# Preparing the next batch item in TensorE's gaps, with routing spread over the attention loop

## The chip, the cores and the metric

The kernel runs on one core of a Trainium2 chip. The metric is the device time of one execution, in microseconds. The kernel before takes 2810.74 us (median of three runs, 2806.79 to 2811.39). The profiled execution has a span of 2745.2 us on the trace and 2746.91 us as a run.

## The reference

Eight items of 256 channels by 1024 positions (32 x 32) pass through two layers, all in f32. Layer 0 is an attention with 8 heads of 64, whose softmax runs over the query axis (`axis=1`). Layer 1 is a single-head attention on a layer norm, and then a mixture of 8 experts, of which each token takes two.

```python
# layer 0
xt = x.reshape(B, C, S).transpose(0, 2, 1)
qkv = (xt @ w_qkv + b_qkv).reshape(B, S, N_HEADS, 3 * D_K)
q, k, v = jnp.split(qkv, 3, axis=-1)
attn = jnp.einsum('bihd,bjhd->bijh', q, k) * SCALE
attn = jax.nn.softmax(attn, axis=1)
res = jnp.einsum('bijh,bjhd->bihd', attn, v).reshape(B, S, N_HEADS * D_K)
x = res @ w_out + b_out + xt
# layer 1
t = t + attention(ln(t), W)           # scores (ln(t) W^T) ln(t)^T, softmax over the last axis
n = ln(t)
probs = softmax(n @ router_w.T); rw, re = top_k(probs, 2); rw = rw / rw.sum(-1)
out = n + sum_e combine[:, e] * (gelu(n @ w1[e] + b1[e]) @ w2[e] + b2[e])
t = t + out
```

## The kernel before

The items are worked on one after the other. Items 0 to 6 are routed: their normed rows are scattered by expert into a table in HBM, and the experts run on all of them together, after layer 0 of item 7. Item 7 itself goes through all eight experts densely. For each item, `layer0`, `attend` and `dispatch` follow each other.

The first part of layer 0 makes the values (4 parts of 2 blocks) and the queries and keys of the first pair of heads. `big` is a PSUM tile of 128 x 1024 f32, and its pool has three buffers; `acc` is 128 x 512, and its pool has two.

```python
def project(b, xT, g, t):                       # t = 0: queries, 1: keys
    pq = big(f"pqk_{b}_{g}_{t}")
    for cc in range(NCC):
        for n in range(NH2):
            nc.tensor.matmul(pq[:, ts(n, 512)], wqkv[:, cc, t, ts(g, P)],
                             xT[:, cc, ts(n, 512)], start=(cc == 0), stop=(cc == NCC - 1))
    dst = two.tile([P, S], F32, tag=f"qk{t}", ...)
    evicted[b, g, t] = nc.vector.tensor_scalar(
        dst, pq, b_qk[:, t, g : g + 1], SCALE if t == 0 else 1.0, ALU.add, ALU.mult)

def values(b, xT):
    v = one.tile([P, NT, INNER], F32, tag="v", name=f"v_{b}")
    for i in range(0, NT, 2):
        pv = big(f"pv_{b}_{i}")
        ...                                     # 4 matmuls 128x128 by 128x512
        for j in range(2):
            nc.vector.tensor_add(v[:, i + j, :], pv[:, ts(j, 512)], b_v)
```

Then come 32 steps (4 pairs of heads by 8 blocks of keys). Each step has two heads `h`; the scores of a head fill a `big` tile in two halves of 512. Two matmuls of 64 rows on different halves of the array run together: the first half of one head's scores beside the second half of the other's. The maximum is taken in two instructions, one for each half; the second continues from the first and gives the bias of the exponential, which also sums its rows.

```python
for at in range(last + LAG + 1):                # LAG = 2
    if at <= last:
        score(at, 0, 0)                         # head 0, first half
    if 0 < at <= last + 1:
        score(at - 1, 1, 1)                     # head 1 of the step before, second half
        soften(at - 1, 1)                       # second max, exponential, 1/sum, vs = v / sum
    if at <= last:
        first_max(at, 0)
        score(at, 0, 1)
        score(at, 1, 0)
        soften(at, 0)
        first_max(at, 1)
    if at >= LAG:
        gather_values(at - LAG)                 # 4 matmuls po <- vs, ex
    if at <= last:
        if g + 1 < NPAIR and j in (3, 5):       # next pair of heads
            qks[g + 1].append(project(b, xT, g + 1, len(qks[g + 1])))
```

After the loop the output projection (`pr`, 8 blocks) gives `t1`. `attend` norms it, transposes it, multiplies with W and runs 8 blocks of attention:

```python
layer_norm(t1, n1, 1e-5, f"a{b}")               # bn_stats, Sqrt on ScalarE, reciprocal, 8 tensor_scalar
to_channels(n1, nT, f"n1_{b}")                  # 16 transposes on TensorE, 2 copies on VectorE
... px -> xa                                    # 8 matmuls
def mix(i, ex, ssum):
    pt = big(f"pa_{b}_{i}")
    ...                                         # 8 transposes of ex
    nc.vector.tensor_copy(aT, pt)
    py = acc(f"py_{b}_{i}")
    ...                                         # 8 matmuls aT x n1
```

`dispatch` norms and transposes again, computes the router's logits with 16 matmuls of 128x8 and then, on small tiles of 128x64 and 128x8, softmax, the two best experts and the row of each token. Two matmuls count rows (`pc` before this token, `pn` in all), in two `acc` tiles. 16 indirect DMAs then scatter the rows.

```python
layer_norm(t2, n2, 1e-5, f"f{b}")
to_channels(n2, nT, f"n2_{b}")
gate, hots = gates(b, nT)                       # logits, Exp on ScalarE, some 20 small VectorE operations
both = hots[0] + hots[1]
pc = before^T both ; pn = ones^T both           # two matmuls, acc tiles
... per, upto (scan), rows, counts
for k in range(2): ... row, exp, to, at         # 6 small VectorE operations each
16 x nc.gpsimd.indirect_dma_start(rows at `at` <- n2)
nc.gpsimd.tensor_add(t2, t2, n2)
nc.sync.dma_start(group.sums[...], t2)
```

Of the kernel before, what the change touches and what calls it, by code (L numbers as in the profile page):

```python
# [10 lines left out]
F32 = mybir.dt.float32  # L11
# [7 lines left out]
def kernel(  # L19
# [23 lines left out]
    nc = tc.nc  # L43
# [241 lines left out]

    def values(b, xT):
        v = one.tile([P, NT, INNER], F32, tag="v", name=f"v_{b}")
        for i in range(0, NT, 2):
            pv = big(f"pv_{b}_{i}")
            for j in range(2):  # L290
                for cc in range(NCC):
                    nc.tensor.matmul(  # L292
                        pv[:, ts(j, 512)],
                        xT[:, cc, ts(i + j, P)],
                        wqkv[:, cc, 2, :],
                        start=(cc == 0),
                        stop=(cc == NCC - 1),
                    )
            for j in range(2):
                nc.vector.tensor_add(v[:, i + j, :], pv[:, ts(j, 512)], b_v)  # L300
        return v

    def layer0(b, xT):

        v = values(b, xT)
        res = one.tile([P, NPAIR, S], F32, tag="res", name=f"res_{b}")
        qks = [[project(b, xT, 0, t) for t in range(2)]]  # L310
        if b == 0:
            prepare()
        steps = [(g, j) for g in range(NPAIR) for j in range(NT)]
        LAG = 2
        pss, firsts, nmaxes, exps, sums, vss = {}, {}, {}, {}, {}, {}
        po = None
# [23 lines left out]
        def soften(at, h):  # L340
# [3 lines left out]
            if h == 0:  # L344
                sums[at] = small.tile([P, 2], F32, tag="sums", name=f"sums_{b}_{g}_{j}")
            nmax = small.tile([P, 1], F32, tag="nmax", name=f"nmax_{b}_{g}_{j}_{h}")
            nc.vector.tensor_scalar(  # L347
                scrap,
# [45 lines left out]
        for at in range(last + LAG + 1):  # L394
            if at <= last:
                score(at, 0, 0)
            if 0 < at <= last + 1:
                score(at - 1, 1, 1)
                soften(at - 1, 1)
            if at <= last:  # L400
                first_max(at, 0)
                score(at, 0, 1)
                score(at, 1, 0)
                soften(at, 0)
                first_max(at, 1)
            if at >= LAG:
                gather_values(at - LAG)
            if at <= last:
                g, j = steps[at]
                if g + 1 < NPAIR and j in (3, 5):  # L410
                    if j == 3:
                        qks.append([])
                    qks[g + 1].append(project(b, xT, g + 1, len(qks[g + 1])))


# [14 lines left out]

    def attend(b, t1, step=lambda i: None):
        n1 = one.tile([P, NT, D], F32, tag="n", name=f"n1_{b}")
        layer_norm(t1, n1, 1e-5, f"a{b}")
        nT = one.tile([P, NCC, S], F32, tag="nT", name=f"nT_{b}")
        to_channels(n1, nT, f"n1_{b}")
# [33 lines left out]

        def mix(i, ex, ssum):  # L470
            pt = big(f"pa_{b}_{i}")
            for m in range(NT):
                nc.tensor.transpose(pt[:, ts(m, P)], ex[:, ts(m, P)], ident)  # L473
            aT = two.tile([P, S], F32, tag="tr", name=f"aT_{b}_{i}")
            nc.vector.tensor_copy(aT, pt)  # L475
            py = acc(f"py_{b}_{i}")
            for m in range(NT):
# [20 lines left out]

    def gates(b, nT):

        pl = acc(f"pl_{b}")
        for i in range(NT):
            for dc in range(NCC):
# [5 lines left out]
                    stop=(dc == NCC - 1),  # L509
                )  # L510

        def tmp(tag):
# [4 lines left out]

        pl3 = pl[:, : NT * E].rearrange("p (i e) -> p i e", e=E)
        m = col("g_m")
        nc.vector.tensor_reduce(m, pl3, AX.X, ALU.max)  # L520
        p = tmp("g_p")
        nc.vector.tensor_sub(p, pl3, bcast(m, E))
        nc.scalar.activation(p, p, AF.Exp)
        z = col("g_z")
        nc.vector.tensor_reduce(z, p, AX.X, ALU.add)
        nc.vector.reciprocal(z, z)
        nc.vector.tensor_mul(p, p, bcast(z, E))

        def first_of_max(src, tag):
            top, best = col(f"{tag}_top"), col(f"{tag}_best")  # L530
            hot = tmp(f"{tag}_hot")
            nc.vector.tensor_reduce(top, src, AX.X, ALU.max)
            nc.vector.tensor_tensor(hot, src, bcast(top, E), ALU.is_equal)
            nc.vector.tensor_mul(hot, hot, rank)
            nc.vector.tensor_reduce(best, hot, AX.X, ALU.max)
            nc.vector.tensor_tensor(hot, hot, bcast(best, E), ALU.is_equal)
            return top, hot

        top1, hot1 = first_of_max(p, "g_1")
        rest = tmp("g_rest")  # L540
        nc.vector.scalar_tensor_tensor(rest, hot1, -2.0, p, ALU.mult, ALU.add)
        top2, hot2 = first_of_max(rest, "g_2")
        total = col("g_total")
# [23 lines left out]

    def dispatch(b, t2, group):

        n2 = one.tile([P, NT, D], F32, tag="n", name=f"n2_{b}")  # L570
        layer_norm(t2, n2, 1e-5, f"f{b}")
        nT = one.tile([P, NCC, S], F32, tag="nT", name=f"n2T_{b}")
        to_channels(n2, nT, f"n2_{b}")
        gate, hots = gates(b, nT)

        def tmp(tag):
# [4 lines left out]
        nc.vector.tensor_add(both, hots[0], hots[1])  # L581
        pc = acc(f"pc_{b}")
        flat = both.rearrange("p i e -> p (i e)")
        nc.tensor.matmul(pc[:, : NT * E], before, flat, start=True, stop=True)
        pn = acc(f"pn_{b}")
        nc.tensor.matmul(pn[:, : NT * E], ones, flat, start=True, stop=True)
# [9 lines left out]
            ALU.add,  # L596
        )
        rows = tmp("d_rows")
        nc.vector.tensor_sub(rows.rearrange("p i e -> p e i"), upto, per)
# [13 lines left out]
        kept = []  # L613
        for k in range(2):
            hot = hots[k]
            sel = tmp("d_sel")
# [4 lines left out]
            exp = keep.tile([P, NT], F32, tag=f"exp{k}", name=f"exp{k}_{b}")  # L621
            nc.vector.tensor_reduce(exp, sel, AX.X, ALU.add)
            to = small.tile([P, NT], F32, tag="d_to", name=f"d_to_{b}_{k}", bufs=2)
            nc.vector.scalar_tensor_tensor(to, exp, float(group.cap), row, ALU.mult, ALU.add)
# [3 lines left out]
        for i in range(NT):  # L628
            for k in range(2):
# [7 lines left out]
                )  # L637

        nc.gpsimd.tensor_add(t2, t2, n2)  # L639
        nc.sync.dma_start(group.sums[group.items.index(b)], t2)  # L640
        group.kept[b] = gate, [(row, exp) for row, exp, _ in kept]
# [254 lines left out]
    def dense(b, t2, step):  # L896
# [15 lines left out]
        for e in range(NWB):  # L912
            weights(e)
        n2 = one.tile([P, NT, D], F32, tag="n", name=f"n2_{b}")
        layer_norm(t2, n2, 1e-5, f"f{b}")
        nT = one.tile([P, NCC, S], F32, tag="nT", name=f"n2T_{b}")
        to_channels(n2, nT, f"n2_{b}")

        nc.gpsimd.tensor_add(t2, t2, n2)
        gate, hots = gates(b, nT)  # L920

# [84 lines left out]
        collect(*pending)  # L1006

    for b in range(B):
        xT = next_x
        if b + 1 < B:  # L1010
            next_x = load_x(b + 1)
        t1 = layer0(b, xT)
        if b + 1 < B:
            t2 = attend(b, t1)
            dispatch(b, t2, groups[0])
            continue
# [10 lines left out]

        t2 = attend(b, t1, lambda i: step(early, i))
        dense(b, t2, lambda i: step(late, i))
# [43 lines left out]
```

## Time and profile before

| what | where it is read | value |
|---|---|---|
| time, median of 3 | the runs | 2810.74 us |
| span of the profiled run | page, head | 2745.2 us |
| mean granted TensorE clock | cores | 0.983 |
| first layer-0 score matmuls of items 2 and 3 | timeline | 612.45, 902.15 |
| a layer-0 matmul group, x8 passes | timeline, first layer of item 3 | 1.99 us (scores), 1.94 us (products) |
| score matmuls psc in all | groups | 581.0 us, 2048 passes |
| product matmuls po in all | groups | 495.9 us, 2048 passes |
| exponential of a head | groups | 1109 ns |
| first-half max, second-half max | groups | 687 ns, 747 ns |

How to read it: an f32 matmul appears as two instructions (passes), so 8 instructions in a row of the timeline are 4 matmuls of the code. The timeline joins equal instructions that follow each other on one engine; its bracket gives the idle time of the engine before the first of them and what ended it. The length of a matmul row includes the time in which it flows through the array, so rows of TensorE overlap by a little; the distance between starts is the better measure. The granted clock stands in the page as tenths for 40 slices, and for any stretch in the table of stretches. Line numbers are those of the kernel before: L273 project, L292 values, L324 scores, L335 and L347 the two maxima, L357 the exponential, L382 the products, L420 and L424 the output projection, L202 to L209 the layer norm, L218 and L219 transposes and their copies, L441 px, L456 to L483 the attention of layer 1, L504 the logits, L520 to L626 routing.

### The profile page before, as it was taken

Reading aid. Unit: us, or ns where it says so; the run is one execution under the profiler, and the core shown is the slowest. Engines: PE = TensorE matmul, PEld = TensorE weight load, DVE = VectorE, ACT = ScalarE, POOL = GpSimd, SP = SyncE. Lnnn points to the kernel's source line nnn. Section 1 sums busy time; section 2 is a strip of 40 time slices with the busy share of each in tenths; the row PEclk is TensorE's granted clock in tenths of the full one; section 3 lists DMA queues with packets and bytes.
Section 4 is the critical chain, followed back from the end, with each engine's and each line's share of the span. In section 5 each row is a group of like instructions: output and inputs, shape, how many; then the busy total and the mean of one; then the engine's idle time right before and its main releaser. Section 6 shows DMA issues by size and latency. Waiting matters only on the chain.

```text
span 2745.2 us, 27697 instructions
## 1 busy us (share of the span) xinstructions
PE 2617.9 (95%) x10153; PEld 1378.9 (50%) x10153; DVE 1539.6 (56%) x3667; ACT 841.2 (31%) x1455; POOL 385.7 (14%) x383
## 2 busy tenths in 40 slices
PE   8999899989999999999999999899989999999899
PEld 3345433653356335633464346433653377776566
DVE  4764566456744665466645764566456753334544
ACT  2441155114521443134312541145114521111122
POOL 0000200020000200020002000200020024444652
PEclk9999999999999999999999999999999999999999
DMA  6992100000000000010001000100010135553542
GB/s 232 385 340 47 62 1 1 16 35 12 1 16 16 31 1 16 10 37 1 16 0 46 1 1 16 46 1 1 0 37 10 41 125 180 180 178 103 177 141 97
DMA packets 82512, 182.37 MB, mean 66 GB/s; under 512 B 15016, under 2 KB 24904, under 8 KB 80584
## 3 DMA queue, kind: packets, MB, share of 16 engines
q1 hardware_dynamic: 57368, 118.65, 12.1%
q0 software_dynamic: 25008, 61.95, 7.3%
q8 instruction: 80, 1.31, 0.2%
q14 instruction: 56, 0.46, 0.1%
HBM read 100.49 MB, written 110.90 MB: 77 GB/s over the span
## 4 chain that ended last, share of the span: by engine, by line
PE 83%; issue 8%; DVE 4%; ACT 3%; DMA 0%; POOL 0%; ACTq 0%; SPq 0%; DVEq 0%
PE psc L324 20%; PE po L382 17%; PE pqk L273 8%; PE py L478 8%; PE ps L456 7%; PE pv L292 5%; PE pr L420 4%; PE px L441 2%; PE pdh L950 2%; PE pdy L974 2%; PE pt_n L218 2%; PE pa L473 2%; PE pe L798 1%; PE pl L504 1%; ACT hb L783 1%
## 5 line engine op out<-in xcount | busy, mean ns | idle before, releaser
L357 ACT ACTIVATE ex<-psc,nmax 128x1024 f32<-128x1024 f32 x512 | 565.8, 1109 | 784.8 <-DVE scrap L347 776.7
L324 PE MATMUL psc<-qk,qk 64*128 64x512 f32 x2048 | 581.0, 624 | 16.8 <-DVE qk L281 11.0
L382 PE MATMUL po<-ex,vs 128*64 128x512 f32 x2048 | 495.9, 605 | 6.6 <-DVE vs L366 6.6
L335 DVE TENSOR_REDUCE nmax<-psc 128x1 f32<-128x512 f32 x512 | 351.3, 687 | 155.7 <-PE psc L324 155.5
L324 PEld LDWEIGHTS psc<-qk,qk 64*128 64x128 f32 x2048 | 229.8, 185 | 363.4 <-ACT ex L357 177.2
L347 DVE TENSOR_SCALAR_CACHE_REDUCE scrap<-psc,nmax 128x512 f32<-128x512 f32 x512 | 382.3, 747 | 37.5 <-PE psc L324 8.0
L382 PEld LDWEIGHTS po<-ex,vs 128*64 128x64 f32 x2048 | 124.8, 136 | 346.5 <-issue 182.7
L639 POOL TENSOR_TENSOR t<-t,n 128x2048 f32<-128x2048 f32 x7 | 31.6, 4513 | 1767.0 <-issue 1476.1
L478 PE MATMUL py<-n,aT 128*128 128x256 f32 x1024 | 241.5, 390 | 10.9 <-DVE aT L475 10.9
L456 PE MATMUL ps<-nT,xa 128*128 128x512 f32 x512 | 236.9, 593 | 0.0
L273 PE MATMUL pqk<-xT,wqkv 128*128 128x512 f32 x512 | 233.9, 602 | 0.4
L478 PEld LDWEIGHTS py<-n,aT 128*128 128x128 f32 x1024 | 194.0, 194 | 67.7 <-DVE aT L475 42.5
L281 DVE TENSOR_SCALAR qk<-pqk,b_qk 128x1024 f32<-128x1024 f32 x64 | 82.2, 1284 | 186.7 <-PE pqk L273 186.7
L467 ACT ACTIVATE ex<-ps,nmax 128x1024 f32<-128x1024 f32 x64 | 71.3, 1114 | 333.6 <-DVE nmax L464 325.4
L273 PEld LDWEIGHTS pqk<-xT,wqkv 128*128 128x128 f32 x512 | 93.4, 190 | 141.0 <-issue 99.4
L483 DVE SCALAR_TENSOR_TENSOR t<-py,rs,t 128x256 f32<-128x256 f32 x64 | 31.0, 484 | 230.9 <-PE py L478 230.9
L292 PE MATMUL pv<-wqkv,xT 128*128 128x512 f32 x256 | 137.5, 687 | 9.2 <-ACT wqkv L97 7.3
L798 PE MATMUL pe<-wb,hb 128*128 128x256 f32 x504 | 125.4, 392 | 10.9 <-ACT hb L783 10.8
L456 PEld LDWEIGHTS ps<-nT,xa 128*128 128x128 f32 x512 | 93.4, 190 | 79.0 <-issue 72.7
L632 POOL DMA_INDIRECT rows<-n,d_at x112 | 109.0, 973 | 151.2 <-DVE row L619 119.2
L842 POOL DMA_INDIRECT yk<-y,yat x112 | 112.6, 1005 | 98.5 <-DVE o L869 52.2
L420 PE MATMUL pr<-wo,res 128*128 128x256 f32 x512 | 121.9, 381 | 0.0
(171 smaller groups left out, 2479.3 us busy)
## 6 DMA issues: line engine op xcount, KB each, us to landing
rows<-wb SPq DMA_DIRECT2D x7, 8192.0 KB, 52.0
y<-yb SPq DMA_DIRECT2D x63, 256.0 KB, 2.0
xT<-in_x_dram SPq DMA_DIRECT2D x7, 1024.0 KB, 4.9
sums<-t SPq DMA_DIRECT2D x7, 1024.0 KB, 4.4
o<-sums SPq DMA_DIRECT2D x7, 1024.0 KB, 6.5
out_dram<-oT SPq DMA_DIRECT2D x14, 512.0 KB, 7.9
wpack<-in_L_ffn_w_dram SPq DMA_DIRECT2D x4, 1024.0 KB
wb<-in_L_ffn_w_dram SPq DMA_DIRECT2D x16, 256.0 KB, 5.4
```

Of the source, the lines that this page charges most:

```text
L273: nc.tensor.matmul(pq[:, ts(n, 512)], wqkv[:, cc, t, ts(g, P)], xT[:, cc, ts(n, 512)], start=(cc == 0), stop=(cc == NCC - 1),)
L292: nc.tensor.matmul(pv[:, ts(j, 512)], xT[:, cc, ts(i + j, P)], wqkv[:, cc, 2, :], start=(cc == 0), stop=(cc == NCC - 1),)
L324: mm = nc.tensor.matmul(pss[at, h][:, ts(n, 512)], k[r, ts(j, P)], q[r, ts(n, 512)], start=True, stop=True)
L335: firsts[at, h] = nc.vector.tensor_reduce(nmax, pss[at, h][:, ts(0, 512)], AX.X, ALU.max, negate=True)
L347: nc.vector.tensor_scalar(scrap, ps[:, ts(1, 512)], -1.0, nmaxes.pop((at, h)), ALU.mult, ALU.min, accum_out=nmax,)
L357: nc.scalar.activation(ex, ps, AF.Exp, bias=nmax, scale=1.0, accum_out=sums[at][:, h : h + 1])
L382: nc.tensor.matmul(po[n][h * DK : (h + 1) * DK, :], vs[:, h, :], exs[h][:, ts(n, 512)], start=(j == 0), stop=(j == NT - 1),)
L420: nc.tensor.matmul(pr[:, :C], res[:, g, ts(i, P)], wo[:, g, :], start=(g == 0), stop=False)
L456: nc.tensor.matmul(psc[:, ts(n, 512)], xa[:, ec, ts(i, P)], nT[:, ec, ts(n, 512)], start=(ec == 0), stop=(ec == NCC - 1),)
L478: nc.tensor.matmul(py[:, :D], aT[:, ts(m, P)], n1[:, m, :], start=(m == 0), stop=(m == NT - 1))
L798: nc.tensor.matmul(py[:, ts(r, D)], hT[:, fc, ts(r, P)], wb[:, at + fc * D : at + (fc + 1) * D], start=(fc == 0), stop=(fc == NFC - 1),)
L842: nc.gpsimd.indirect_dma_start(out=yk[:, i, k, :], out_offset=None, in_=self.group.y[:, :], in_offset=bass.IndirectOffsetOnAxis(ap=ats[k][ ...
```

## The change

Four things are moved; apart from the copy named below, what is computed stays the same.

1. **The next item's beginning in gaps.** Values and the first two projections of item b+1 are no longer made at the start of its layer 0. `attend` and the norm before routing of item b call them at named places: the queries' projection after the first norm, values part 0 ahead of the last block's transposes and part 1 ahead of its products, parts 2 and 3 after the second norm, the keys' projection after the logits. The purpose is to give TensorE work while it waits for VectorE or ScalarE.
2. **Routing in steps.** `gates` and `dispatch` become generators, and one step of them is issued in each step of the next item's layer-0 loop, behind its first-half maximum of head 1. The logits are first copied to SBUF (one more VectorE copy of 128x64). The two counts share one `big` tile instead of two `acc` tiles, which the products of layer 0 use at that time.
3. **Order of the maxima.** `issue_after` places the second-half max of head 1 of the step before ahead of the first-half max of head 0, and the second-half max of head 0 ahead of the first-half max of head 1.
4. **The sum t2 + n2** and its store are issued before routing.

```diff
+        def at(self, place):
+            if place == "norm 1":
+                self.project()
+            elif place == "last weights":
+                self.values(0)
+            elif place == "last products":
+                self.values(1)
+            elif place == "norm 2":
+                self.values(2)
+                self.values(3)
+            elif place == "logits":
+                self.project()
 ... (layer0)
-        v = values(b, xT)
+        v, qks = begun.v, begun.qks
-        qks = [[project(b, xT, 0, t) for t in range(2)]]
-            nc.vector.tensor_scalar(
+            seconds[h] = nc.vector.tensor_scalar(
 ...
             if at <= last:
-                first_max(at, 0)
+                with tc.issue_after(seconds[1].ins) if 1 in seconds else nullcontext():
+                    first_max(at, 0)
                 score(at, 0, 1)
                 score(at, 1, 0)
                 soften(at, 0)
-                first_max(at, 1)
+                with tc.issue_after(seconds[0].ins):
+                    first_max(at, 1)
 ...
+                with tc.issue_after(firsts[at, 1].ins):
+                    next(routing, None)
+        for _ in routing:
+            pass
 ... (attend)
         layer_norm(t1, n1, 1e-5, f"a{b}")
+        fill("norm 1")
 ...
+            if i == NT - 1:
+                fill("last weights")
             pt = big(f"pa_{b}_{i}")
 ...
             nc.vector.tensor_copy(aT, pt)
+            if i == NT - 1:
+                fill("last products")
 ... (gates, dispatch: generators with yields)
+        l = small.tile([P, NT, E], F32, tag="g_l", name=f"g_l_{b}", bufs=1)
+        nc.vector.tensor_copy(l.rearrange("p i e -> p (i e)"), pl[:, : NT * E])
 ...
-        pc = acc(f"pc_{b}")
+        pcn = big(f"pcn_{b}")
+        pc, pn = pcn[:, :512], pcn[:, 512:]
-        pn = acc(f"pn_{b}")
 ... (main loop)
-            t2 = attend(b, t1)
-            dispatch(b, t2, groups[0])
+            begun = Begin(b + 1, next_x)
+            t2 = attend(b, t1, begun.at)
+            n2, _, l = normed(b, t2, begun.at)
+            nc.sync.dma_start(groups[0].sums[b], t2)
+            routing = dispatch(b, n2, l, groups[0])
```

## The prediction

> **What bounds the kernel now.** I read the busy shares and the chain first, then the timeline of one item, then the granted clock. An item's period is about 289 us (first score matmuls at 612.45 and 902.15). Busy shares and chain, from the page:
>
> ```profile
> PE 2617.9 (95%) x10153; PEld 1378.9 (50%) x10153; DVE 1539.6 (56%) x3667; ACT 841.2 (31%) x1455; POOL 385.7 (14%) x383
> ...
> PE 83%; issue 8%; DVE 4%; ACT 3%; DMA 0%; POOL 0%; ACTq 0%; SPq 0%; DVEq 0%
> ```
>
> TensorE sets the time; its matmul instructions cannot be fewer after this change. What can be won is time in which it stands, or runs at half clock. The timeline between two items shows both:
>
> ```profile
> 572.07 3.72 PE L478 MATMUL py<-n,aT 128*128 128x256 f32 x16 [1.40 <-DVE aT L475]
> 578.27 3.92 PE L218 MATMUL pt_n<-ident,n 128*128 128x128 f32 x16 [2.48 <-DVE n L209]
> 588.90 10.34 PE L292 MATMUL pv<-wqkv,xT 128*128 128x512 f32 x18
> 612.45 3.70 PE L324 MATMUL psc<-qk,qk 64*128 64x512 f32 x12 [1.38 <-DVE qk L281]
> 590.00:592.00 2.00, 2.00 (x4) 0.91 (x3) 0.00 (x0) 0.00 (x0) 0.00 (x0) 0.50 0.00 0
> ```
>
> Columns: start, length, engine, line, operation, count, and in brackets the idle time and its releaser; the last line is the table of stretches, where 0.50 is the granted clock. TensorE waits 1.40 us for the copy of the attention weights, 2.48 us for the norm, 1.38 us for the last projection; and the values' matmuls take 0.86 us a pass instead of 0.43 until 593.3. The first norm:
>
> ```profile
> 785.65 0.20 DVE L207 RECIPROCAL rstd_a<-rstd_a 128x8 f32<-128x8 f32 x1 [0.27 <-ACT rstd_a L206]
> 786.05 2.67 DVE L209 TENSOR_SCALAR n<-t,mv_a,rstd_a 128x256 f32<-128x256 f32 x8 [0.20 <-DVE rstd_a L207]
> 786.52 4.02 PE L218 MATMUL pt_n<-ident,n 128*128 128x128 f32 x16 [2.49 <-DVE n L209]
> 790.57 7.66 PE L441 MATMUL px<-nT,WT 128*128 128x512 f32 x16
> ```
>
> Inside layer 0, one step:
>
> ```profile
> 935.90 1.99 PE L324 MATMUL psc<-qk,qk 64*128 64x512 f32 x8
> 937.06 0.69 DVE L335 TENSOR_REDUCE nmax<-psc 128x1 f32<-128x512 f32 x1 [0.99 <-PE psc L324]
> 937.67 0.74 DVE L347 TENSOR_SCALAR_CACHE_REDUCE scrap<-psc,nmax 128x512 f32<-128x512 f32 x1
> 938.51 1.11 ACT L357 ACTIVATE ex<-psc,nmax 128x1024 f32<-128x1024 f32 x1 [1.93 <-DVE scrap L347]
> 939.77 0.30 PEld L324 LDWEIGHTS psc<-qk,qk 64*128 64x128 f32 x4 [0.89 <-ACT ex L357]
> ```
>
> The next step's scores wait for a PSUM buffer that this exponential frees: 1.16 us to the first-half max, 0.61 to the second-half one, 0.84 with its accumulator, 1.11 for the exponential, 0.15 on: 3.87. TensorE's own work, taken where nothing waits, is 1.92 (scores, 935.90 to 937.82) and 1.87 (products, 934.03 to 935.90): 3.79. Steps take 3.87 and 4.01 in turn, so they lose only 0.15.
>
> **What the Trainium skill says.** "TensorE: Matmul & The Clock Gate", Part 1: the array runs at half clock after about 3.4 us of low activity and needs as long to recover; Part 4 adds that transposes do not count as busy. The trace agrees: 0.50 follows each gap with transposes. The same page, Part 3 (the mechanism): matmuls start and end in program order; so a matmul that waits holds up all behind it, which matters for the routing counts below. "ScalarE: Activation LUTs", What ACT_TABLE_LOAD costs: about 1283 ns, and some 1380 ns of drain. The trace has the 1.28 us, but the exponential starts at once after it (803.01 + 1.28, next start 804.30), without a drain:
>
> ```profile
> 577.46 1.28 ACT L523 ACT_TABLE_LOAD   x1
> ...
> 803.01 1.28 ACT L467 ACT_TABLE_LOAD   x1 [17.39 <-DVE nmax L464]
> ```
>
> The first load runs before its operand is there; the second takes over the wait of the exponential that follows and is fully exposed.
>
> **The change, part by part.** I also read the order in which the changed program issues its instructions on each engine. Seven transitions are concerned (items 0 to 6 each prepare the next one). Values are 4 parts and projections 2, each 4 matmuls of two passes at 0.43 us: 3.44 us a part, 20.6 us in all.
>
> *First norm.* One of the four projection matmuls moves into the 0.90 us gap at the end of layer 0 (before 1054.21), three follow the last output projection: 2.58 us. But on VectorE the eviction of the projection (1.28 us) is issued ahead of the reciprocal. It can start 2.78 us after the last output matmul and ends at 4.06; normalising starts at 4.5 instead of 2.0. So px starts 2.5 us later. Of 3.44 us filled, 0.9 are won.
>
> *Last attention block.* Two parts, 6.88 us, go in. They fill 1.74 us (the wait for the last exponential, seen at 855.59) and most of the 1.40 us copy wait. Tracing the order by hand from the end of py 6: 1.72 (rest of the first part), 1.03 (transposes), 3.44, 3.72, so py 7 ends at 9.9 instead of 5.9: 4.0 us later.
>
> *Second norm to first score.* Before: 575.79 to 612.45, 36.7 us. After: two parts to 6.9; 16 transposes to 9.0; VectorE adds the bias of the last part until 8.45 and then copies the transposes to 9.7 and 10.95; three projection matmuls and 16 router matmuls (0.23 us each, from 1.85 us for 16 passes) lie between 9.0 and 16.4; the last matmul to 17.2; eviction 1.28 and latencies: scores at 18.5. That is 18.2 us less.
>
> Sum of a transition: 18.2 - 4.0 - 2.5 = 11.7. Part of the half clock stays (transposes, tiny router matmuls); I take off 0.7: **11.0 us**.
>
> *Table load.* The exponential table is now loaded ahead of the first exponential of layer 0, with its wait: exposed as at 803.01. Before, TensorE waited there for that exponential already (612.45 to 616.58). Loss 1.3 us an item.
>
> *Routing in steps.* Some 40 VectorE operations of 0.16 to 0.29 us go into steps 0 to 12 of layer 0. A step of the new order costs VectorE about 3.45 us (0.68 + 0.72 + 0.78 + 0.19 + 0.60 + 0.32, and 0.1 to 0.2 waiting for the row sums) against 3.79 of TensorE, so 0.5 us of room. Steps with 0.75 to 0.9 us of routing lose 0.3 to 0.6; those with a projection lose nothing: 1.8 us an item.
>
> *Counts matmuls.* Two small matmuls (0.8 us with their latency) stand in TensorE's order before the next step's scores. They need an operation that VectorE reaches at about 4.8 us in the step, where TensorE is free at 3.8: 1.1 us of standing. Their tile also holds one of three PSUM score buffers for a step, so scores lose their pairing. Followed by hand, three steps take 14.7 us instead of 11.4: 3.3 us an item.
>
> *Order of the maxima.* The second-half max goes first, so the chain above loses the 0.61 of the other max: 3.26, under TensorE's 3.79. The 0.15 us a step goes, not the 0.58 after each projection (scores wait there for the eviction). Steps that are not next to a projection lost 2.7 us an item; in items with routing I count 2.0.
>
> Sum: 7 x (11.0 - 1.3 - 1.8 - 3.3 + 2.0) + 2.7 = 7 x 6.6 + 2.7 = **49 us**. The timed median is 2810.74, the profiled span 2745.2; I take the difference off unchanged: 2762.
>
> **Rivals.** (1) *Everything won is kept.* If neither routing nor table load shows, because VectorE is 56% busy and catches up in projection steps, it is 7 x 13 + 2.7 = 94 us: 2717. For it: the loop's slack. Against: layer 0's waits all pass through VectorE and ScalarE, and the counts matmul blocks in order. (2) *VectorE becomes the bound of layer 0.* If its steps cost 4.0 rather than 3.45, with 0.5 more in 32 steps of 8 items, 128 us are lost and the kernel is slower: 2890. Against: measured back to back, the same operations in the old order need 3.24 (647.36 to 650.60). A milder form, lateness carried from step to step, costs perhaps 20 us: 2782. (3) *The clock.* If the new gaps still drop it for full windows at both norms, 2 us more an item: 2776; if the gaps are dense enough, 2 us less. (4) *Transfers.* Row scatters come later, with 16 issues of about 1.27 us; they have all of layer 0 and are hidden.
>
> **Range and chances.** The transition is the surest term (11 +- 2, times 7); the losses inside layer 0 add up to 6.4 an item, with an uncertainty of 3. Together about 19 us of spread: 2738 to 2786. The 2% line lies at 2754.5, a little under my value: 36% faster, 61% within, 3% slower.
>
> **What would show it.** Right: from the last product of attention to the first score 18 to 19 us; px about 9 us after the last output projection; the table load in front of the first layer-0 exponential with a wait in brackets; a gap of about 1 us before the counts matmuls; steps of 3.8 us in the second half of layer 0. Wrong: loop steps above 3.9 without routing (rival 2), or px not later than before, or a clock of 0.5 after the second norm.

## The result and the profile after

The changed kernel takes **2738.25 us** (median of four runs, 2737.5 to 2740.61), beside 2808.76 for the kernel before (four runs, 2804.14 to 2811.39): a ratio of 0.9752, 95% interval 0.9735 to 0.9769. The prediction said 2762, with a range that began at 2738. The value lies on that lower edge.

One fact is needed to read all that follows. Different runs were placed on different chips, and these fall into two kinds: on one (**kind A**) the kernel before takes 2746 us, on the others (**kind B**) 2809 to 2828. Each chip was used in one session only, so the chip and the hour are not told apart. The profile of before that the prediction was worked out from behaves as kind A; the recorded times of before and after are of kind B. So a ratio is given here only between runs of one chip, and periods of single items are compared where no disturbance of kind B lies in them.

The busy shares and the chain of the changed kernel (page):

```profile
PE 2620.2 (96%) x10153; PEld 1370.5 (50%) x10153; DVE 1518.2 (55%) x3675; ACT 865.5 (32%) x1455; POOL 388.8 (14%) x383
...
PE 86%; issue 7%; DVE 4%; ACT 2%; DMA 0%; another core or an unknown queue 0%; POOL 0%; ACTq 0%; SPq 0%; DVEq 0%
```

TensorE bounds it as before; its share of the chain went from 83% to 86%. The timeline of TensorE in the changed kernel between two items:

```profile
575.48 3.62 PE L527 MATMUL py<-n,aT 128*128 128x256 f32 x16
578.93 7.03 PE L304 MATMUL pv<-wqkv,xT 128*128 128x512 f32 x16
...
585.80 1.91 PE L218 MATMUL pt_n<-ident,n 128*128 128x128 f32 x16
...
590.52 3.41 PE L553 MATMUL pl<-rT,n2T 128*128 128x8 f32 x30
...
596.27 5.28 PE L361 MATMUL psc<-qk,qk 64*128 64x512 f32 x12 [1.38 <-DVE qk L281]
```

The waits of 1.40 us for the weights' copy and 2.48 us for the norm no longer stand in brackets: values of the next item fill them. From the end of the last product (579.1) to the first score it is 17.2 us instead of 33.7 to 36.9. But the first scores now take 5.28 us for twelve passes, not 3.70. The first norm of the changed kernel (timeline):

```profile
776.66 1.28 DVE L281 TENSOR_SCALAR qk<-pqk,b_qk 128x1024 f32<-128x1024 f32 x1 [1.27 <-PE pqk L273]
...
778.56 3.05 PE L218 MATMUL pt_n<-ident,n 128*128 128x128 f32 x16 [1.93 <-DVE n L209]
...
782.71 9.35 PE L486 MATMUL px<-nT,WT 128*128 128x512 f32 x16 [1.10 <-DVE nT L219]
```

The eviction of the projection stands ahead of the norm, as predicted, and px begins 8.7 us after the last output projection, instead of 6.5. It then takes 9.35 us instead of some 7.8.

The start of layer 0 in the changed kernel (timeline):

```profile
600.70 1.28 ACT L394 ACT_TABLE_LOAD   x1 [19.95 <-DVE scrap L384]
...
603.25 5.49 PE L361 MATMUL psc<-qk,qk 64*128 64x512 f32 x10 [1.71 <-ACT ex L394]
```

The clock in both places, from the table of stretches (columns: stretch, length, busy time with count of PE, PEld, DVE, ACT and POOL, granted clock, DMA share, GB/s; the first line is the stretch of the first norm):

```profile
780.00:787.00 7.00, 5.90 (x13) 2.78 (x13) 3.11 (x5) 0.00 (x0) 0.00 (x0) 0.53 0.00 0
...
596.00:600.00 4.00, 3.73 (x9) 1.87 (x10) 1.04 (x3) 0.00 (x0) 0.00 (x0) 0.57 0.00 0
600.00:603.00 3.00, 1.54 (x4) 0.37 (x2) 2.85 (x8) 2.29 (x2) 0.00 (x0) 0.98 0.00 0
603.00:610.00 7.00, 6.75 (x14) 3.40 (x16) 4.87 (x16) 4.27 (x10) 0.00 (x0) 0.52 0.00 1
```

px runs at half clock for most of its time. At the start of layer 0 the table's load waits in front of the first exponential, TensorE stands 1.71 us for it, and two stretches at half clock lie over the first scores, one on each side of that wait. Further on, the counts (timeline):

```profile
638.80 0.22 DVE L650 TENSOR_TENSOR d_both<-g_hot,g_hot 128x64 f32<-128x64 f32 x1
...
639.16 0.41 PE L654 MATMUL pcn<-d_both,before 128*128 128x64 f32 x2 [0.71 <-DVE d_both L650]
```

TensorE stands 0.71 us until VectorE has added the two choices.

### The profile page after: what moved, and what is told of

The parts are those of the page before. It is cut to its first block, busy times and chain, and to the rows that moved or that the text cites. A ratio compares the mean times of both kernels' runs of the same rounds, so it can differ in the third digit from the quotient of the medians.

```text
span 2738.9 us, 27857 instructions
## 1 busy us (share of the span) xinstructions
PE 2620.2 (96%) x10153; PEld 1370.5 (50%) x10153; DVE 1518.2 (55%) x3675; ACT 865.5 (32%) x1455; POOL 388.8 (14%) x383
## 4 chain that ended last, share of the span: by engine, by line
PE 86%; issue 7%; DVE 4%; ACT 2%; DMA 0%; another core or an unknown queue 0%; POOL 0%; ACTq 0%; SPq 0%; DVEq 0%
PE psc L361 20%; PE po L419 17%; PE pqk L273 8%; PE py L527 8%; PE ps L501 6%; PE pv L304 4%; PE pr L464 4%; PE px L486 3%; PE pe L867 2%; PE pdy L1044 2%; PE pdh L1020 2%; PE pa L520 2%; PE ph L842 2%; PE pt_n L218 1%; PE pl L553 1%
## 5 line engine op out<-in xcount | busy, mean ns | idle before, releaser
L361 PE MATMUL psc<-qk,qk 64*128 64x512 f32 x2048 | 599.6, 649 | 24.5 <-ACT ex L394 13.4
L419 PE MATMUL po<-ex,vs 128*64 128x512 f32 x2048 | 506.7, 609 | 0.3 <-DVE vs L403 0.3
L273 PE MATMUL pqk<-xT,wqkv 128*128 128x512 f32 x512 | 240.3, 606 | 0.0
L304 PE MATMUL pv<-wqkv,xT 128*128 128x512 f32 x256 | 119.4, 610 | 9.2 <-ACT wqkv L97 7.0
```

What stands on the lines that cost most here:

```text
L304: nc.tensor.matmul(pv[:, ts(j, 512)], self.xT[:, cc, ts(i + j, P)], wqkv[:, cc, 2, :], start=(cc == 0), stop=(cc == NCC - 1),)
L361: mm = nc.tensor.matmul(pss[at, h][:, ts(n, 512)], k[r, ts(j, P)], q[r, ts(n, 512)], start=True, stop=True)
L419: nc.tensor.matmul(po[n][h * DK : (h + 1) * DK, :], vs[:, h, :], exs[h][:, ts(n, 512)], start=(j == 0), stop=(j == NT - 1),)
```

## The experiments

Periods and loops below are worked out from the timelines: a period runs from an item's first score to the next item's, a loop from the first score to the end of the last product of layer 0. Mean periods are over the seven routed items; mean loops are over items 1 to 6, in which the routing or the scatters of the item before fall.

**1. Before, unchanged (kind A).**

> The kernel before, unchanged, profiled once more. Its recorded profile has 2746.9 us, while its timed runs have 2804 to 2811, 62 us more; the changed kernel's profile agrees with its timed runs. Theory A (the tail): the recorded profile of before escaped stalls in the last item's part after the experts, where the gathers of expert results are issued; it took 237 us there, and the changed kernel took 263 with stalls of up to 9.7 us. Then a profile of about 2806 shows 290 to 300 us there, and the same item periods as before (286.7 to 290.1). Theory B (the clock): the timed runs are spread with more half-clock windows in each item; then the item period is 293 to 297 us instead, the mean granted clock is about 0.96 instead of 0.983, and the part after the experts is unchanged at 237. If the profile is again near 2747, it is the profiled execution that differs from a timed one, and neither is told apart.

Measured: 2746.26 us, 1.000 of before (interval 0.9991 to 1.0008). The profile repeats the recorded one: periods of 287.6 us on average, 692.9 for the last item. All 27 executions there took 2742 to 2748 us, so the 62 us were not a matter of luck in one execution. They go with the chip, and this run could not show where they lie.

**2. Order of the maxima alone (kind A).**

```
 first_max(at, 0)   ->  issued after the second-half max of the other head (seconds[1])
 first_max(at, 1)   ->  issued after seconds[0]
```

> Before, with only the order of the maxima changed: the second-half max and its exponential ahead of the next first-half max. Prediction's step: 0.15 us a step off in steps not next to a projection, 2.7 us an item, 8 items: 22 us under before (ratio 0.992). Rival: VectorE's order makes no difference where TensorE's own work is 3.79 us a step, since half of it comes back as waits in front of the scores: within 6 us of before. A second rival: the order matters more than the steps show, because it also lets TensorE recover from each projection (0.58 us): 40 us under before.

Measured: 2719.43 us, 0.9897 (0.9873 to 0.9921), 26 us under before. The loop falls from 154.1 to 152.0 us; a pair of steps goes from 3.87 + 4.02 to 3.79 + 3.90, and one with a projection from 7.50 to 7.42. px falls from 7.8 to 7.1. Of the prediction's 2.7 us an item, all of which it had put into the loop, the loop gives 2.1 and px the other 0.7.

**3. After, without that order (kind A).**

```
-with tc.issue_after(seconds[1].ins) ...: first_max(at, 0)
+first_max(at, 0)                                  # both maxima
```

> After, with the maxima in the order of before. If the prediction's step is right, it is 17 us over after (2.0 us an item in seven items and 2.7 in one): 2755. If the order of the maxima is what hides the routing's small VectorE operations, more: 2770 to 2790. If the order does nothing, 2738.

Measured: 2714.85 us, 0.9889 (0.9872 to 0.9905). Held against the periods of after (from a chip of kind B, but free of its waits in these items), the order gains nothing here: 281.97 us on average without it, 282.09 with it. The loop is 1.6 us longer without it (161.7 against 160.1), but px takes 7.13 us instead of 9.3. What the order saves in the loop is lost again as half clock at the next norm. Where the half clock falls seems to be a matter of timing and not of the order as such: in the changed programs of experiments 7 and 8, px takes 7.13 us in some items and 8.9 to 9.4 in others. That the order causes it is not shown.

**4. After, with the routing at once ahead of layer 0 (kind A).**

```
-routing = dispatch(b, n2, l, groups[0])
+for _ in dispatch(b, n2, l, groups[0]): pass
```

> After, with the routing run to its end ahead of layer 0 instead of in its steps; values and projections stay in the gaps. By the prediction the steps lose 1.8 us of routing and 3.3 us of counts matmuls an item, which go, but the routing's chain of some 40 small operations (about 15 us on VectorE, with the counts matmuls standing in front of the scores in TensorE's order) comes ahead of the first score: 7 x (15 - 5.1) = 69 us over after: 2807. Rival: the routing's chain runs beside the last values and projections, which TensorE needs 10 us for: only 5 us more an item, less 5.1: about 2738. Second rival: the wait drops the clock for two more windows (3.4 us each, half lost): 2830.

Measured: 2695.44 us, 0.9818 (0.9801 to 0.9834). The mean period is 279.7 us, under the 282.1 of after. The price before the first score is 5.3 us (22.5 against 17.2), not 15: most of the chain runs beside the last projection and the router. In return the loop loses its 6 us of routing, start and counts (153.9 against 160.1). The table is loaded right behind the second norm's root, where nothing waits, and the counts now stand in front of the scores (timeline of this version):

```profile
575.29 1.28 ACT L577 ACT_TABLE_LOAD   x1
...
594.64 0.66 PE L654 MATMUL pcn<-d_both,before 128*128 128x64 f32 x2 [5.21 <-DVE d_both L650]
```

The rival was near: spreading the routing is no gain by itself on this chip; it costs about 2.4 us an item.

**5. After, unchanged, again (kind B).**

> The changed kernel, unchanged. On the chip of its first record it took 2738 and the kernel before 2809; the runs since then show before at 2746 with the same periods of its items, 287.7 us, so before lost 62 us on that chip outside what its profile shows. Theory: the work on the seven items costs the same everywhere (periods of 283.3, as in its first profile), and the 26 us that its first profile loses after the last item's layer 0, against 237 us of before, go: 2700 to 2708, ratio 0.984. Rival: those 26 us belong to the order of the maxima or to the smaller dense part and come back: 2738, ratio 0.997.

Measured: 2742.59 us beside 2810.18, 0.9762 (0.9705 to 0.9818): the first result again, on a chip of the same kind. The periods of the first record are repeated (283.3). Neither theory could be tested there; after was not run on a chip of kind A.

**6. First part of the routing ahead (kind B).**

```
 routing = dispatch(b, n2, l, groups[0])
+next(routing)                 # maximum, difference, exponential
```

> After, with the first part of the routing (maximum, difference, exponential) ahead of layer 0. The exponential table is then loaded right behind the second norm's root, where nothing waits for it. The first three steps of layer 0 take 15.3 us in after and 10.5 with the order of the maxima alone, 4.7 more. Theory of the table alone (the prediction's term): 1.3 us an item less, 7 x 1.3 = 9 us under after. Theory of the clock: the table's load makes TensorE stand 1.7 us, and that calls down a second window at half clock of 6.8 us; without the load the window goes too, 3.4 to 4.5 us an item, 24 to 32 us under after. Theory of the cold start: the half clock comes from the gap and the small router matmuls before the first scores; then only the 1.3.

Measured: 2769.11 us, 0.9861 (0.9806 to 0.9916), 27 us **over** after. At the start of layer 0 all went as hoped: the first three steps take 12.6 us on average, not 15.2, and that is more than the 1.3 of the table. But the whole routing, with its scatters, is a step earlier, and step 13 of layer 0 takes 14.5 to 16.1 us instead of 7.4; the loops of items 1 to 6 are 165.5 to 166.1 us instead of 160. VectorE idles in each of them for 3.4 to 8.1 us, for matmuls that had ended before (timeline):

```profile
952.82 2.07 PE L361 MATMUL psc<-qk,qk 64*128 64x512 f32 x6
...
959.38 0.75 DVE L384 TENSOR_SCALAR_CACHE_REDUCE scrap<-psc,nmax 128x512 f32<-128x512 f32 x1 [4.07 <-remote]
```

The scores end at 954.9; the maximum that reads them starts at 959.38, after 4.07 us of idle time ("remote": ended by something that this core's profile does not show). Such waits are what experiment 9 looks for in before.

**7. Counts a step later (kind B).**

```
 nc.vector.tensor_add(both, hots[0], hots[1])
+yield
 pcn = big(f"pcn_{b}")
```

> After, with the two counts matmuls one step later than the operation that they wait for, so that they never stand in TensorE's order. The steps around them take 3.25 us more than without them. Prediction's split: 1.1 us of standing (and the seven-tenths seen in brackets) goes, the 2.2 us for the score buffer stay: 7 x 1.1 = 8 us under after. Rival: it is the standing alone that costs, and the buffer is free: 7 x 3 = 21 us under after. Second rival: only the buffer costs: same as after.

Measured: 2732.58 us, 10 us under after of the same chip (0.9738 against 0.9762 of before, intervals that overlap). The two steps around the counts take 4.77 + 5.83 instead of 5.12 + 5.83; without counts they are 3.79 + 3.91. So the standing costs 0.35 us; what remains, 2.9, is put down to the score buffer, which was not tried alone: nearer to the second rival than to the prediction's split, though the sum of 3.25 is the predicted 3.3. Seven times 0.35 is 2.5 of the 10 us; the rest lies in px (8.6 us on average instead of 9.3) and in the last item (724.9 instead of 729.4), which the edit does not touch.

**8. Both, 6 and 7 (kind B).** The edits are those two.

> Both of the former: first part of the routing ahead of layer 0, counts matmuls a step later. If the two are independent, the sum of their gains. By the clock theory and the standing of 1.1: 7 x (4 + 1.1) = 36 us under after; by the table alone and 1.1: 17 us under. It is the version in steps that could beat the routing done at once, whose seven periods are 279.7 us against 282.2 of after: to do so it needs more than 18 us.

Measured: **2719.07 us**, 0.969 (0.9637 to 0.9744) of before and 23.5 us under after on the same chip. It beats both kernels. The first three steps take 12.7 us on average, the counts 10.6 in two steps, and the long step of experiment 6 is gone.

**9. Before, on a chip of kind B.**

> The kernel before once more, for a profile where it takes 2810 and not 2746. The profiles of the changed kernel and its variants show waits of VectorE and ScalarE that end with a semaphore from TensorE long after the matmul had ended, 3 to 14 us each, only where GpSimd issues indirect transfers, and only on the chip where before takes 2810: 42 to 52 us in the changed kernel, all in the last item, and 90 in the variant with the first part of the routing ahead, where 36 of them fall on the scatters inside layer 0. Theory A: before has about 64 us of such waits there, some in each item's scatters (which come beside the first scores and projections) and the rest in the last item: item periods of 290 to 294 instead of 287.7 and 710 to 730 us for the last item instead of 692.9. Theory B: its items are unchanged at 287.7 and the whole 64 us are in the last item: 757 us. Theory C: it is the granted clock: periods up and no such waits. If it takes 2746 again, there are none of these waits, and periods as before.

Measured: 2820.72 us, 1.000 of before on that chip. Theory A holds, with periods up to 297.1 us even more than it said: its loops take 158.8 to 162.4 us from item 1 on, instead of 154.1, and item 7's 164.4 instead of 156.2; the last item is 727.4 instead of 692.9. Theory C is not the start of it: the granted clock is 1.00 where the waits begin, and falls behind them. First item 3 on kind A (timeline of TensorE, experiment 1), then the same steps here (timeline, and the table of stretches):

```profile
912.56 1.94 PE L382 MATMUL po<-ex,vs 128*64 128x512 f32 x8
914.51 3.70 PE L273 MATMUL pqk<-xT,wqkv 128*128 128x512 f32 x8
918.14 2.57 PE L324 MATMUL psc<-qk,qk 64*128 64x512 f32 x8
```

```profile
916.48 0.75 DVE L347 TENSOR_SCALAR_CACHE_REDUCE scrap<-psc,nmax 128x512 f32<-128x512 f32 x1 [2.71 <-issue]
...
917.91 0.97 POOL L632 DMA_INDIRECT rows<-n,d_at  x1 [0.30 <-issue]
...
918.59 1.98 PE L324 MATMUL psc<-qk,qk 64*128 64x512 f32 x6 [1.26 <-ACT ex L357]
...
923.55 2.07 PE L324 MATMUL psc<-qk,qk 64*128 64x512 f32 x2 [2.98 <-ACT ex L357]
...
925.55 3.68 PE L382 MATMUL po<-ex,vs 128*64 128x512 f32 x8
...
933.07 1.28 DVE L281 TENSOR_SCALAR qk<-pqk,b_qk 128x1024 f32<-128x1024 f32 x1 [6.33 <-PE pqk L273]
...
907.00:918.00 11.00, 9.65 (x30) 3.60 (x30) 5.99 (x15) 4.17 (x7) 8.26 (x10) 1.00 0.28 96
918.00:933.00 15.00, 11.44 (x26) 3.59 (x26) 5.39 (x14) 4.04 (x8) 0.88 (x1) 0.77 0.05 18
```

While GpSimd issues the last scatters, VectorE idles 2.71 us for nothing that the profile shows; everything behind it is late, and the step takes 14.4 us instead of 7.5. Half clock follows: TensorE stands 2.98 us, and the products behind take 3.68 us instead of 1.94. From the granted clock of 0.77 over these 15 us, in which TensorE was busy for 11.44, the half clock is an estimated 3 of the 7 us.

**10. Gates ahead, counts at the end of step 0 (kind B).**

```
 (the yield of 7)
 routing = dispatch(b, n2, l, groups[0])
+for _ in range(8): next(routing)          # up to the counts
```

> After, with the gates (all up to the sum of the two choices) ahead of layer 0 and the counts matmuls at the end of step 0, the rest in steps. The routing done at once costs 5.3 us between the last product and the first score (22.5 against 17.2), because the counts matmuls stand in front of the scores; after loses 3.2 us at the counts in steps 7 and 8, and 4.7 in the first three steps. Theory: gates on VectorE delay the first maxima by 1.5 to 2 us, the table is loaded early (1.3 to 2.5 less), the score buffer costs little while the softmax has yet to fill: period 277 us against 283.3 of after and 279.7 at once, 7 x 6 = 42 us under after: 0.97 x before where before takes 2746, 0.961 x where it takes 2810. Rival: the buffer costs its 2.9 us here as well: 280, no better than at once. Second rival: the first scores lose their pairing and the clock falls at the start: 283 or more, no better than after.

Measured: 2746.58 us, 0.9738 (0.969 to 0.9786), no better than after. The mean period is 282.3. The first three steps take 9.3 + 5.5 + 4.3 = 19.1 us (timeline, and the table of stretches):

```profile
889.44 0.66 PE L655 MATMUL pcn<-d_both,before 128*128 128x64 f32 x2 [4.52 <-DVE rs L401]
...
876.00:893.00 17.00, 11.10 (x30) 5.51 (x31) 9.11 (x35) 2.67 (x5) 0.00 (x0) 0.50 0.00 1
```

The second rival was right, and above all in its clock: TensorE stands 4.52 us in front of the counts, while VectorE works off the gates, and the clock is 0.50 over the 17 us around that.

**11. Routing at once, on a chip of kind B.** The edit is that of 4.

> The version with the routing run at once ahead of layer 0, again, this time to see it on a chip where before takes 2810 to 2820 (its first record, 0.982 of before, is from one where before takes 2746). Its scatters go out from 4 to 24 us after the first score, over the same steps as those of before (from -8 to 12), while those of after go out from 58 to 79 us. Theory of the place: indirect transfers beside the first steps make VectorE stand there on such a chip, as in before (its first-layer loops take 160.3 us there against 154.1), and after wins by having them elsewhere; then the periods here are 285 to 288 instead of 279.7, and it is slower than after: 0.985 of before against 0.976 of after. Rival: the waits do not depend on the place; then the periods stay at 280 and it is 0.968 of before. On a chip where before takes 2746 it repeats 0.982.

Measured: 2795.31 us, 0.9883 (0.985 to 0.9916), against 0.976 for after on this kind. The mean period is 288.5 instead of 279.7. Steps 3 and 4 take 8.8 + 11.9 us here and 7.4 + 4.4 on kind A (timeline):

```profile
911.55 3.70 PE L273 MATMUL pqk<-xT,wqkv 128*128 128x512 f32 x8 [1.34 <-ACT ex L394]
...
920.84 1.28 DVE L281 TENSOR_SCALAR qk<-pqk,b_qk 128x1024 f32<-128x1024 f32 x1 [6.96 <-remote]
...
922.18 2.07 PE L361 MATMUL psc<-qk,qk 64*128 64x512 f32 x2 [5.02 <-DVE qk L281]
```

The projection ends at 915.3; its eviction begins at 920.84, and TensorE waits 5 us for it. GpSimd issues its last scatter at 917.3. The same program that was the fastest of kind A loses to after on kind B.

**12. Before, with direct writes in place of the scatters (kind B).**

```
-nc.gpsimd.indirect_dma_start(out=view, out_offset=at[:, i], in_=n2[:, i, :])
+nc.sync.dma_start(view[fixed rows], n2[:, i, :])      # in the program behind a small write of the indices
```

> Before, with the 16 scattered writes of an item replaced by 16 direct writes of the same size to fixed rows, issued by SyncE after the last index is ready: it leaves out the sorting of rows by expert (the experts then work on other rows), and keeps the bytes and about the time of the transfers. Theory: it is the indirect transfers issued by GpSimd beside the steps that make VectorE stand; on a chip where before takes 2810 to 2820 the loops of layer 0 fall from 160.3 to 154.1 us and the time by 43 us, 0.985 of before, with the last item's 727 us unchanged. Rival: the traffic itself does it: same as before. On a chip where before takes 2746, the same as before within 5 us in either case.

Measured: 2778.43 us, 0.9832 (0.98 to 0.9864), 49.5 us under before of the same chip. It leaves out the sorting of rows by expert. The loops are back at 154.1 us, item 7's at 156.6, and the mean period is 288.2. So the 7 us an item are gone once the scatters are gone from the first steps. The last item keeps 720 us; the gathers there were left as they are.

What it is about the scatters, the run does not tell, because the edit did more than was meant. The direct writes need no indices, and they went out before these were ready (timeline of SyncE; the first score of this item is at 899.81):

```profile
865.27 7.72 SPq L634 DMA_DIRECT2D rows<-n  x16
...
891.05 1.88 SPq L630 DMA_DIRECT2D held<-d_at  x2
```

They are issued 35 to 27 us ahead of the first score, where the scatters of before are issued from 8.5 us ahead of it to 10.7 us behind it. The traffic beside the first steps is gone as well as the indirect transfers, and the rival is not excluded. What speaks against the traffic is after, in experiment 5: there the same rows are scattered beside steps 11 to 14 on kind B, and these steps take within 0.12 us what they take in experiment 2 on kind A. The edit also changed two things at once, the engine that issues and the kind of transfer. The Trainium skill, "DMA: Bandwidth & Descriptors", section SWDGE vs HWDGE vs iDMA, says that for GpSimd's transfers a program writes the descriptors into rings in the on-chip memory, and that those of SyncE never take this path. No run here shows that this has a part in the waits.

## Why the prediction was right, and where it was not

**The step that failed is the last one of the sum**: "I take the difference off unchanged". The 65 us between the profiled span, 2745.2, and the timed median, 2810.74, were taken for a constant that both kernels pay. More than half of them are a cost of before that the change removes. On kind B the scatters of before cost 49 us up to the end of item 7's layer 0 (experiments 1 and 9: its first score comes at 2091.8 us instead of 2050.9, and its loop is 8.2 us longer), and 46 of these go when the scatters go from there (experiment 12). In after they cost nothing that can be seen: loops of 160.1 us on kind B, and 161.7 on kind A in experiment 3, where the order of the maxima is missing. Rival 4 had asked only whether the scatters are hidden after the change, and there it was right; whether they had been hidden before was not asked. What both kernels do pay on kind B is the attention and dense part of the last item, with its gathers: 263 us against 237, in both. Nothing in the profile of kind A could show the 49 us, but the gap between its span and the timed median was there as a warning.

**The items gained less than predicted.** Before on kind A and after, per item:

| term of the sum | predicted | measured | from |
|---|---|---|---|
| last product to first score | +18.2 | +17.4 | 34.6 to 17.2 |
| last attention block | -4.0 | -3.4 | 67.0 to 70.4 |
| px later | -2.5 | -2.2 | loop end to px, 24.1 to 26.3 |
| rest of the half clock | -0.7 | -1.5 | px itself, 7.8 to 9.3 |
| table load, first three steps | -1.3 | -4.7 | 10.55 (maxima alone) to 15.24 |
| routing's small operations | -1.8 | -0.2 | steps 9 to 12 |
| counts matmuls | -3.3 | -3.25 | steps 7 and 8, 7.70 to 10.95 |
| order of the maxima | +2.0 | +2.1 | experiment 2 |
| sum | +6.6 | +4.3 | periods 287.6 and 283.3 |

Six of the eight terms hold within 0.8 us. In the first, two errors nearly cancel: the item that was read had 36.7 us before, the mean is 34.6, and the 18.5 expected after came out as 17.2. **The mis-sized one is the start of layer 0, booked as the table load**: the load itself is 1.28 us, but TensorE meets half clock over the first scores, and the term is 4.7. Part of it comes ahead of the load: the first six passes take 2.72 us instead of 1.39. In experiment 4, with the load early and no routing in the steps at all, the three steps still take 12.5 us. Experiments 6 and 8 take the load out of the way and get 2.5 to 2.6 back; the other 2.1 stay. The Trainium skill, "TensorE: Matmul & The Clock Gate", Part 1, gives an idle window of about 3.4 us as what halves the clock. Here TensorE was busy for 1.54 of the 3.00 us from 600 to 603, with a stand of 1.71 us, and half clock followed over nearly all of 603 to 610: less than a whole idle window was enough. The small operations cost only 0.2 us in steps 9 to 12; those in the first three steps are not told apart from the clock.

By spans, after gains 38.9 us up to item 7's first score and gives 7.0 back in its loop, which now holds the routing of item 6: **32 us, where 49 were predicted**. The other 49 us are the scatters of before. Together 81, against 80.3 between the two profiled spans of kind B (2819.2 and 2738.9), and 70.5 between the medians of the recorded chip, where before was about 10 us quicker than in that profile. So the number came out inside the range by luck: a sum that was 17 us too high and a missing term of some 40, with opposite signs, at the very edge of the range. The likeliest class of the prediction, within 2%, did not come; the gain was 70.5 us and not 49. On a chip of kind A the change is worth an estimated 32 us, 0.988, within 2%; that was not run, but experiment 3, all of the change except the order of the maxima, gave 31 us there.

Rival 1 (everything kept) was wrong: of its 94 us two thirds were lost again. Rival 2 was wrong: VectorE did not become the bound, steps without routing take 3.79 and 3.90 us. Rival 3 was right in direction: the half clock costs more than was taken off, and the prediction's own sign of being wrong, a clock of 0.5 after the second norm, was there (0.57 from 596 to 600, 0.52 from 603 to 610).

**Where the waits come from is not fully settled.** They go with indirect transfers on kind B; but scatters in layer 0 did not always cost. The line of GpSimd in after (experiment 5), at its ninth scatter:

```profile
948.41 0.97 POOL L704 DMA_INDIRECT rows<-n,d_at  x1 [1.54 <-DVE vs L403]
```

In after, 7, 8 and 10 the second eight indices come later, and in the row of issues, otherwise 1.27 us apart, the ninth starts 2.4 to 3.9 us behind the eighth. In before, 6 and 11 sixteen follow without a break. On kind B the long steps are in those three programs and in none of the other four. The place in the loop does not decide it: the unbroken row of 6 runs from 51 to 71 us after the first score, the broken one of 8 from 55 to 76. That fits a backlog of unbroken issues, and would make the routing in steps worth its cost by accident; a break alone was not tried, nor was it seen what distinguishes the chips.

## What to carry to other kernels

Compare the span of a profile with the timed runs before using it: if they differ by per cents, the profile lacks a cost that the result will contain. When an operation moves to another engine's path, add to its own length the wait that it makes on TensorE and the clock that falls around it. Small indirect transfers can cost time even if their bytes seem hidden: take the stage once with them and once without, on the chip whose time counts, and look in the trace at when each variant really issues them.

## What was not expected of the hardware

- The same program differs by 62 to 82 us between chips. In the profiles of experiments 1 and 9 VectorE and ScalarE are equally busy (1538.7 and 842.0 us, 1539.8 and 842.0); TensorE is busy 32 us longer (2616.7 and 2648.8), at a granted clock of 0.984 and 0.970. The difference begins in waits of 2 to 14 us on VectorE and ScalarE, for matmuls that had ended, and they were found only beside indirect transfers of GpSimd.
- Sixteen indirect writes of 128 rows, issued without a break, cost the kernel about 7 us an item on such a chip; sixteen direct writes of the same bytes, at an earlier place, cost nothing that can be seen (loops of 154.1 us).
- Two matmuls of 64 columns cost 2.9 us even where they never stand; the likely cause is the tile of scores that they hold for a step.
- Half clock comes in stretches of 3.4 us or multiples of it, up to 17 in experiment 10. The order of the maxima won 26 us alone and, by its periods, nothing within the whole change, where px fell into half clock.
